# A transformer block with 4-bit FFN weights: attention ordered by rising row blocks over all heads, QKV by chunks of rows, twelve row blocks projected inside the attention loop

## The chip, the core and the metric

The kernel runs on one core of a Trainium2 chip. The metric is the device time of one execution in microseconds; lower is better. The core's engines, each with its own instruction stream that it works through in order, are TensorE (PE in the profile; its weight loads stand apart as PEld), VectorE (DVE), ScalarE (ACT) and GpSimd (POOL). SyncE (SP) issues all DMAs of this kernel, in one order; 16 DMA engines carry them out.

## The reference

One transformer block in fp32 on x of 2048 rows by 1024 columns: causal attention with 16 heads of 64, rotary positions, then a gated FFN (inner width 2752) whose weights are 4-bit codes with a table of 16 values and a scale for each 64 of them.

```python
q, k, v = (layernorm(x) @ W).reshape(2048, 16, 64)   # for each of Wq, Wk, Wv
q, k = rotary(q), rotary(k)
attn = softmax(where(causal, q @ k.T, -1e9) / 8)
x = x + layernorm((attn @ v) @ Wo)
Wg, Wu, Wd = (NF4[codes] * scales)                    # 64 values share a scale
x = x + layernorm((silu(layernorm(x) @ Wg.T) * (layernorm(x) @ Wu.T)) @ Wd.T)
```

## The kernel before

**Products of three.** An fp32 operand is split into a high part in TensorE's rounded fp32 type (ACT copies it) and a low part (DVE or POOL subtracts). `split` (L130) does both. A product is three matmuls: high by high, high by low, low by high. The 128x512 matmul is the unit of everything.

**Buffers.** SBUF is cut into tagged slots (L71): `hd`, `w`, `xc`, `pa` of 8 KB per partition, `pb`, `f4`, `pw` of 4 KB, `t2` and `ol` of 2 KB, so many of each; a tile waits until a slot of its tag is free. The eight PSUM banks have tags too (L72): one `F` for QKV and projection, three `S` for scores, two `T` for maxima, row sums and transposes, one `O` and one `L` for the attention output and its low-part sum. A planning pass puts each engine's instructions in order by priority and readiness; the function `chain` (L333) fixes the order of TensorE's matmuls by hand through the whole attention loop.

**Start, 0 to about 190 us.** `make_x` (L197) normalises and transposes the four chunks of 512 rows of x into resident tiles and stores them to DRAM (`xd`). `prep_qkv` (L217) loads and splits the weight columns of a pair of heads `m`; pairs 0 and 1 are computed here for all four chunks. `qkv(m, c)` (L222) is a group: for each of q, k, v 24 matmuls into `F`, a copy, then rotary for q and k (DVE shuffle L251, multiply L252, POOL L253 and L254) or four transposes for v, the split, and a store to DRAM.

**The attention loop, about 190 to 1630 us.** It has 640 steps. A step is one unit `(h, J, kb)`: head `h`, query block `J` of 512 rows, key block `kb` of 128. Order (L286): head by head, `J` rising inside a head; only for the last pair of heads is `J` outside. In each step, in this order: `probabilities` (L373; two score matmuls into `S`, on the diagonal a mask matmul, exp on ACT, the split into `pw`, POOL's addition into `acc`), one `maxima` chunk (L341; a score matmul into `T`, DVE's maximum) for a block some 16 steps ahead, a share of filling matmuls, and `weighted` (L401; matmuls into `O` and `L`) for the unit two steps before. At a block's end the two banks are added (L415, L416) and stored to `at`, and the row sums follow by two matmuls. K and V of a head lie in two sets of tiles; `load_block` (L305) adds only the new 512 rows for each `J`.

The filling (`rest`, L490) is a generator: the groups of pairs 2 to 7, each reading its x chunk again from `xd` (`load_x`, L210), with the next pair's weights split along the way; then the output projection of the first four row blocks (`project`, L450: load `at`, multiply by the reciprocal sums, split, 48 matmuls, and `residual`, L475: layernorm, sum with x, layernorm, stores `x1d` and `yd`). A `GAP` ends a step's share. At most 6 matmuls a step are taken, 3.35 on average.

**Between loop and FFN, about 1630 to 1866 us.** `project_now` projects the other twelve row blocks; between them `fill_x2` loads finished blocks from `yd` and transposes them into the FFN's input tiles, and the first gate and up weight tile is decoded (`looked_up`, L574).

**FFN, from about 1866 us.** For each of 22 weight tiles 4 chunks of products, while DVE and ACT decode the next tile; then the down projection and the last residual.

Of the kernel before, what the change touches and what calls it, by code (L numbers as in the profile page):

```python
# [20 lines left out]
S = 2048  # L21
# [9 lines left out]
BESIDE = 4  # L31
NEWX = 7
EARLY = 1000
STEP = 4
PACE = 3.35
MOST = 6
LAG = 2
AHEAD = (16, 16, 18, 20)
LOADS = 4
# [19 lines left out]
def block_kernel(ctx, tc, x, wq, wk, wv, wo, gu_codes, gu_scales, d_codes, d_scales, cos_sin, out):  # L59
# [117 lines left out]
    def prep_w(w, m, scale, tag="w"):  # L177

        wf = slot("f4", [P, KE, P], F32, "wf")
        load(wf, w[:, m * P : (m + 1) * P].rearrange("(k p) n -> p k n", p=P))  # L180
        n = KE // 2 if tag == "pb" else KE
        parts = []
        for k0 in range(0, KE, n):
            t = slot(tag, [P, 2, n, P], FR, "w")
            for k in range(0, n, STEP):
                src, hi, lo = wf[:, k0 + k : k0 + k + STEP], t[:, 0, k : k + STEP], t[:, 1, k : k + STEP]
                A.activation(hi, src, AF.Copy, scale=scale)
                if m > 1:
                    V.scalar_tensor_tensor(lo, src, scale, f32(hi), ALU.mult, ALU.subtract)
                else:  # L190
                    if scale != 1.0:
                        G.tensor_scalar(src, src, scale, 0.0, ALU.mult, ALU.add)
                    G.tensor_tensor(lo, src, f32(hi), ALU.subtract)
            parts += [t[:, :, k, :] for k in range(n)]
        return parts

    def make_x(c):  # L197
        tiles = [slot(("pa", "xc", "hd", "xc")[c], [P, 2, 2, 512], FR, "xr") for _ in range(4)]
        for t in range(4):
            r = (4 * c + t) * P  # L200
            xt = slot("hd" if c == 0 or t == 3 else "pw", [P, E], F32, "xt")
            load(xt, x[r : r + P, :])
            mean, rs, _ = ln_stats(halves(xt))
            V.tensor_scalar(xt, xt, mean, rs, ALU.subtract, ALU.mult)
            transposed(xt, tiles, slice(t * P, (t + 1) * P))
        for kp in range(4):
            load(xd[c][:, kp], f32(tiles[kp]))
        return tiles
# [8 lines left out]
    def prep_qkv(m, tags=("w", "w", "w")):  # L217
        return [prep_w(w, m, sc, tag) for w, sc, tag in zip((wq, wk, wv), (0.125, 1.0, 1.0), tags)]
# [3 lines left out]
    def qkv(m, c, ws, xs, ramp=False, following=None):  # L222

        cs = slice(c * 512, (c + 1) * 512)
        tab = slot("f4", [P, 2, 512], F32, "tab")
        load(tab, cos_sin[:, :, cs])
        for n in range(3):
# [8 lines left out]
            A.copy(t1, o)  # L236
            if following:
                following[n] = prep_w((wq, wk, wv)[n], m + 1, (0.125, 1.0, 1.0)[n])
            if n == 2:
                yield GAP  # L240
                pv = bank("F", "pv").rearrange("p (t n) -> p t n", t=4)
# [23 lines left out]

    xs = [early(make_x, 0)]
    first = [early(prep_qkv, 0), prep_qkv(1, ("pa", "pa", "pb"))]

    def new_x(c):
        xs.append(early(make_x, c))  # L270

    def both(*steps):
        for m, c in steps:
            for _ in qkv(m, c, first[m], xs[c], ramp=True):
                pass

    new_x(1)
    both((0, 0), (1, 0))
    new_x(2)
    both((0, 1), (1, 1))  # L280
    new_x(3)
    both((0, 2), (0, 3), (1, 2), (1, 3))


    last = KE - 1
    order = [(h, J) for h in range(2 * last) for J in range(NC)]  # L286
    order += [(h, J) for J in range(NC) for h in (2 * last, 2 * last + 1)]
    units, chunks, begin = [], [], {}
    for h, J in order:
        begin[h, J] = len(units)  # L290
        units += [(h, J, kb) for kb in range(4 * J + 4)]
        chunks += [(h, J, j, i) for j in range(4) for i in range(J + 1)]

    kv_of, q_of, q_free, pw_of, of, done = {}, {}, [], [], {}, set()

    def head_room():

        ka, kb = slot("hd", [P, S], FR, "ka"), slot("hd", [P, S], FR, "kb")
        va, vb = slot("hd", [P, NT, P], FR, "va"), slot("pa", [P, NT, P], FR, "vb")
        G.memset(f32(kb[:D]), 0.0)  # L300
        G.memset(f32(kb[:1]), 1.0)
        G.memset(f32(vb[:, :, D:]), 1.0)
        return ka, kb, va, vb

    def load_block(h, J):  # L305
# [3 lines left out]
        if h < 2 and J == 0:  # L309
            kv_of[h] = head_room()  # L310
        ka, kb, va, vb = kv_of[h % 2]
        for a in range(2):
            load(f32(ka[a * D : (a + 1) * D, cs]), ks[m][r : r + D, a, cs])
        load(f32(kb[D:, cs]), ks[m][r : r + D, 0, cs])
        if len(q_free) < 4 and not any(free for _, free in q_free):
            two = slot("pa", [P, 2, 2, 512], FR, "q")
            G.memset(f32(two[:D, :, 1]), 0.0)
            for i in range(2):
                q_free.append([two[:, i], True])
        entry = next(e for e in q_free if e[1])  # L320
        entry[1] = False
        q_of[h, J] = entry
        q = entry[0]
# [3 lines left out]
        ts = slice(4 * J, 4 * J + 4)  # L327
# [45 lines left out]
    def probabilities(u, h, J, kb):  # L373
# [9 lines left out]
        if kb == 4 * J + 3:  # L383
            q_of[h, J][1] = True
# [443 lines left out]
```

## Time and profile before

| what | value |
|---|---|
| time, median of 3 runs | 3258.65 us (3253.39 to 9025.56) |
| the profiled execution's time | 3266.51 us |
| its span, first to last instruction | 3264.5 us |
| mean granted TensorE clock | 0.965 |
| instructions | 42321 |
| DMA traffic | 569.68 MB, mean 175 GB/s |

Busy time counts the union of an engine's instructions. The heaviest groups of the attention part:

| line, engine | what | times | mean ns |
|---|---|---|---|
| L399 POOL | acc, sum of the high probabilities | 576 | 1144 |
| L353 DVE | row maxima | 640 | 603 |
| L132 DVE | low part of the probabilities | 640 | 603 |
| L385 ACT | exp | 640 | 518 |
| L131 ACT | high part of the probabilities | 640 | 524 |
| L189 DVE | low part of a weight half tile | 36 | 903 |
| L193 POOL | the same for the first two pairs | 12 | 1352 |
| L187 ACT | high part of a weight half tile | 48 | 632 |

DMA issues that the change touches, as the profile lists them: x chunks from `xd` 96 of 1024 KB; rotary tables 32 of 512 KB; weights 24 of 512 KB; `ka` 128, `kb` 64 and `vb` 64 of 128 KB, `va` 64 of 256 KB; x stores 16 of 1024 KB.

How to read it: an engine's row gives its name, busy time, share of the span and number of instructions. A table by stage gives the same for a stretch of time. A wait names who waited, for whom, the sum, how often, and the longest.

### The profile page before, as it was taken

Reading aid. Unit: us, or ns where it says so; the run is one execution under the profiler, and the core shown is the slowest. Engines: PE = TensorE matmul, PEld = TensorE weight load, DVE = VectorE, ACT = ScalarE, POOL = GpSimd, SP = SyncE. Lnnn points to the kernel's source line nnn. Section 1 sums busy time; section 2 is a strip of 40 time slices with the busy share of each in tenths; the row PEclk is TensorE's granted clock in tenths of the full one; section 3 lists DMA queues with packets and bytes.
Section 4 is the critical chain, followed back from the end, with each engine's and each line's share of the span. In section 5 each row is a group of like instructions: output and inputs, shape, how many; then the busy total and the mean of one; then the engine's idle time right before and its main releaser. Section 6 shows DMA issues by size and latency. Waiting matters only on the chain.

```text
span 3264.5 us, 42321 instructions
## 1 busy us (share of the span) xinstructions
PE 3027.4 (93%) x13760; PEld 2460.7 (75%) x13760; DVE 2232.7 (68%) x4037; ACT 1867.0 (57%) x3366; POOL 1008.7 (31%) x899
## 2 busy tenths in 40 slices
PE   8979999999998989968867999999999999999998
PEld 6857777777777767746656788888888888888887
DVE  8457777777777777756646598666677767957422
ACT  3246666666666656665625587555566556747311
POOL 5346666565665656664612100000000000000000
PEclk9989999999999999978978999999999999999999
DMA  8766757566566566453166533222222224868785
GB/s 304 262 194 199 239 157 219 182 186 213 183 190 207 189 180 216 149 142 91 57 174 194 180 117 115 92 97 97 104 97 100 91 99 153 299 206 254 257 290 206
DMA packets 307549, 569.68 MB, mean 175 GB/s; under 512 B 60160, under 2 KB 166656, under 8 KB 281728
## 3 DMA queue, kind: packets, MB, share of 16 engines
q1 hardware_dynamic: 307328, 566.99, 54.6%
q8 instruction: 108, 1.77, 0.2%
q14 instruction: 113, 0.93, 0.1%
HBM read 420.74 MB, written 146.15 MB: 174 GB/s over the span
## 4 chain that ended last, share of the span: by engine, by line
PE 74%; DMA 9%; DVE 8%; issue 4%; ACT 3%; POOL 2%; SPq 1%; DVEq 0%; POOLq 0%; ACTq 0%
PE bk L125 14%; PE bk L126 14%; PE bk L127 14%; PE qkv L232 4%; PE qkv L233 4%; PE qkv L234 4%; PE l L408 3%; PE mx L347 3%; PE o L407 3%; PE s L379 3%; PE s L380 3%; DMA rt<-rc 2%; DVE mxs L353 1%; DVE st L137 1%; DVE pw L132 1%
## 5 line engine op out<-in xcount | busy, mean ns | idle before, releaser
L399 POOL TENSOR_TENSOR acc<-acc,pw 128x512 f32<-128x512 f32 (+3 forms) x576 | 658.8, 1144 | 430.4 <-ACT pw L131 411.5
L591 ACT ACTIVATE ln<-cs,bias 128x512 f32<-128x512 f32 x910 | 611.4, 718 | 135.3 <-DVE mp L597 46.4
L125 PE MATMUL bk<-x,wt 128*128 128x512 f32 x1376 | 535.6, 390 | 0.6 <-DVE x L132 0.5
L126 PE MATMUL bk<-x,wt 128*128 128x512 f32 x1376 | 535.9, 390 | 0.0
L127 PE MATMUL bk<-x,wt 128*128 128x512 f32 x1376 | 535.6, 389 | 0.0
L143 POOL TENSOR_TENSOR rs<-ve,nhalf 128x1 f32<-128x1 f32 x64 | 40.5, 637 | 1560.0 <-DVE ve L141 1559.9
L353 DVE TENSOR_REDUCE mxs<-mx 128x1 f32<-128x512 f32 (+3 forms) x640 | 380.8, 603 | 190.0 <-PE mx L347 109.7
L385 ACT ACTIVATE s<-s 128x512 f32<-128x512 f32 (+3 forms) x640 | 330.7, 518 | 298.7 <-PE s L380 168.8
L132 DVE TENSOR_TENSOR pw<-s,pw 128x512 fp32r<-128x512 f32 (+3 forms) x640 | 383.5, 603 | 133.6 <-ACT pw L131 129.0
L131 ACT CAST pw<-s 128x512 fp32r<-128x512 f32 (+3 forms) x640 | 332.5, 524 | 33.2 <-POOL acc L399 3.1
L125 PEld LDWEIGHTS bk<-x,wt 128*128 128x128 f32 x1376 | 258.6, 188 | 54.7 <-issue 0.8
L126 PEld LDWEIGHTS bk<-x,wt 128*128 128x128 f32 x1376 | 258.7, 188 | 53.7 <-DVE x L132 0.3
L127 PEld LDWEIGHTS bk<-x,wt 128*128 128x128 f32 x1376 | 258.8, 188 | 53.7
L232 PE MATMUL qkv<-xc,w 128*128 128x512 f32 x576 | 238.8, 415 | 60.2 <-issue 42.2
L408 PE MATMUL l<-pw,vb 128*128 128x512 f32 (+3 forms) x640 | 247.0, 386 | 26.2 <-DVE acc L416 19.6
L125 PE MATMUL bk<-wd,it 128*128 128x512 f32 x672 | 261.7, 389 | 0.6 <-DMA it<-ind 0.5
L126 PE MATMUL bk<-wd,it 128*128 128x512 f32 x672 | 261.4, 389 | 0.0
L127 PE MATMUL bk<-wd,it 128*128 128x512 f32 x672 | 261.3, 389 | 0.0
L407 PE MATMUL o<-pw,va 128*128 128x512 f32 (+3 forms) x640 | 243.1, 380 | 16.3 <-ACT pw L131 9.9
L347 PE MATMUL mx<-ka,q 128*128 128x512 f32 (+3 forms) x640 | 246.0, 396 | 9.2 <-DVE mxs L353 6.1
L379 PE MATMUL s<-q,ka 128*128 128x512 f32 (+3 forms) x640 | 243.7, 381 | 3.7 <-DVE pw L132 3.6
L380 PE MATMUL s<-q,kb 128*128 128x512 f32 (+3 forms) x640 | 239.0, 373 | 0.0
(140 smaller groups left out, 5774.6 us busy)
## 6 DMA issues: line engine op xcount, KB each, us to landing
xc<-xd SPq DMA_DIRECT2D x96, 1024.0 KB
it<-ind SPq DMA_DIRECT2D x84, 1024.0 KB
ind<-hl SPq DMA_DIRECT2D x84, 512.0 KB
q<-qs SPq DMA_DIRECT2D x192, 128.0 KB
cs<-in_gu_scales SPq DMA_DIRECT2D x172, 128.0 KB
cs<-in_gu_codes SPq DMA_DIRECT2D x86, 256.0 KB
tab<-in_cos_sin SPq DMA_DIRECT2D x32, 512.0 KB
xd<-xr SPq DMA_DIRECT2D x16, 1024.0 KB
```

Source lines behind the costliest of these rows:

```text
L125: r = T.matmul(o, lhsT=w[:, 0], rhs=xx[:, 0], start=first, stop=False)
L126: T.matmul(o, lhsT=w[:, 0], rhs=xx[:, 1], start=False, stop=False)
L127: T.matmul(o, lhsT=w[:, 1], rhs=xx[:, 0], start=False, stop=last)
L132: V.tensor_tensor(lo, src, f32(hi), ALU.subtract)
L232: yield T.matmul(o, lhsT=w[k][:, 0], rhs=xx[:, 0], start=k == 0, stop=False)
L347: chain(T.matmul(s, lhsT=q[:, 0, j * P : (j + 1) * P], rhs=ka[:, b:e], start=True, stop=not diag))
L353: V.tensor_reduce(mx[:, j, i : i + 1], s, AX.X, ALU.max, negate=True)
L379: chain(T.matmul(s[:, cs], lhsT=ka[:, ks_], rhs=q[:, 0, cs], start=True, stop=False))
L399: G.tensor_tensor(acc[:, cs], acc[:, cs], f32(pw[:, 0, cs]), ALU.add)
L407: chain(T.matmul(o[:, cs], lhsT=va[:, kb], rhs=pw[:, 0, cs], start=kb == 0, stop=end))
L408: chain(T.matmul(ls[:, cs], lhsT=vb[:, kb], rhs=pw[:, 1, cs], start=kb == 0, stop=end))
L591: A.activation(ln, c8, AF.Identity, bias=bias_of[ab], scale=ab[0])
```

## The change

1. **Order of the loop.** `J` is outside for all heads: block 0 of the 16 heads, then block 1, and so on. K and V no longer stay with a head: each block loads its whole past into rings of tiles (`room`), three for `ka`, two each for `kb`, `va`, `vb`; `ka` with q from `load_q`, then `load_k` 8 and `load_v` 5 steps ahead of the block.
2. **QKV.** Groups run chunk by chunk. x of the current chunk stays in the `xc` slots and its rotary table in a `pw` slot. Weights are loaded and split again for every group; low parts of q's weights are subtracted on DVE, those of k's and v's on POOL. The factor 1/8 moves from q's weights to the copy of q. The start makes only x's first chunk and four groups; the other three chunks are made between the loop's steps by a second generator, `other_x`, with its transposes in `chain`, and reach the loop through DRAM. The transposes of v go to bank `T`.
3. **Filling.** 28 groups and the projections of twelve row blocks, at the rate of the table `FILL` (step, matmuls by then), up to 16 in a step. A projection waits four gaps ahead of its matmuls, and its result `y` takes the slot of its input `af`.
4. **Units.** The split of the probabilities (`parts`) comes after the filling; `pw` has three places instead of four; the matmul into `L` goes ahead of that into `O`; 65 rows of `L` are copied by ACT and DVE adds from the copy.
5. **After the loop.** The last four row blocks are projected; the first two gate and up tiles run for chunks 0 and 1 ahead of chunks 2 and 3, whose x2 is filled in between.

```diff
-BESIDE = 4
+BESIDE = 12
-PACE = 3.35
-MOST = 6
+STARTUP = 4
+MOST = 16
+FILL = ((-12, 0), (14, 304), (130, 912), (290, 1520), (430, 2128), (440, 2128), (640, 2704))
...
+        for k in range(0, KE, STEP):
+            src, hi, lo = wf[:, k : k + STEP], t[:, 0, k : k + STEP], t[:, 1, k : k + STEP]
+            A.copy(hi, src)
+            (G if n else V).tensor_tensor(lo, src, f32(hi), ALU.subtract)
...
+    def x_rows(r, tag):
+        xt = slot(tag, [P, E], F32, "xt")
+        load(xt, x[r * P : (r + 1) * P, :])
+        mean, rs, _ = ln_stats(halves(xt))
+        V.tensor_scalar(xt, xt, mean, rs, ALU.subtract, ALU.mult)
+        return xt
...
+    def make_x(c, t):
+        xt = x_rows(4 * c + t, "f4")
+        for _ in range(3):
+            yield GAP
+        for g in range(0, KE, 4):
+            pt = bank("T", "pt").rearrange("p (k n) -> p k n", k=4)
+            for k in range(4):
+                yield T.transpose(pt[:, k], xt[:, (g + k) * P : (g + k + 1) * P], ident)
+            for k in range(0, 4, 2):
+                xs = slot("t2", [P, 2, 2, P], FR, "xs")
+                split(xs[:, 0], xs[:, 1], pt[:, k : k + 2])
+                load(xd[c][:, (g + k) // 2, :, :, t * P : (t + 1) * P], f32(xs))
+            yield GAP
...
-                pv = bank("F", "pv").rearrange("p (t n) -> p t n", t=4)
+                pv = bank("T", "pv").rearrange("p (t n) -> p t n", t=4)
...
-    order = [(h, J) for h in range(2 * last) for J in range(NC)]
-    order += [(h, J) for J in range(NC) for h in (2 * last, 2 * last + 1)]
+    order = [(h, J) for J in range(NC) for h in range(2 * KE)]
...
+    rings = {"ka": [3, 0, []], "kb": [2, 0, []], "va": [2, 0, []], "vb": [2, 0, []]}
...
+        ka = room("ka", h, J)
+        for a in range(2):
+            load(f32(ka[a * D : (a + 1) * D]), ks[m][r : r + D, a, : cs.stop])
...
+    def load_k(h, J):
+        m, r = h // 2, h % 2 * D
+        load(f32(room("kb", h, J)[D:]), ks[m][r : r + D, 0, : J * 512 + 512])
+
+    def load_v(h, J):
+        m, cs = h // 2, slice(0, J * 512 + 512)
+        load(f32(room("va", h, J)), vs[m][cs, h % 2, :].rearrange("(t p) n -> p t n", p=P))
+        load(f32(room("vb", h, J)[:, :, :D]), vs[m][cs, h % 2, :D].rearrange("(t p) n -> p t n", p=P))
...
+        if not pw_of:
+            two = slot("pa", [P, 2, 2, 512], FR, "pw")
+            pw_of.extend([two[:, 0], two[:, 1], slot("pb", [P, 2, 512], FR, "pw3")])
+        pw = pw_of[u % 3]
...
+        chain(T.matmul(ls[:, cs], lhsT=vb[:, kb], rhs=pw[:, 1, cs], start=kb == 0, stop=end))
         chain(T.matmul(o[:, cs], lhsT=va[:, kb], rhs=pw[:, 0, cs], start=kb == 0, stop=end))
-        chain(T.matmul(ls[:, cs], lhsT=vb[:, kb], rhs=pw[:, 1, cs], start=kb == 0, stop=end))
...
+        low = slot("ol", [D + 1, 512], F32, "low")
+        A.copy(low, ls[: D + 1, :])
         A.copy(y, o[D:, :])
-        low = slot("ol", [1, 512], F32, "low")
-        A.copy(low, ls[D : D + 1, :])
         V.tensor_tensor(y, o[:D, :], y, ALU.add)
-        V.tensor_tensor(y, ls[:D, :], y, ALU.add)
+        V.tensor_tensor(y, low[:D, :], y, ALU.add)
...
-        yield GAP
+        y = y if y is not None else af.rearrange("p k n -> p (k n)")
+        for _ in range(4):
+            yield GAP
...
+    groups = [(m, c) for c in range(NC) for m in range(KE)]
+
+    def other_x():
+        for c in range(1, NC):
+            while c > 1 and (0, c - 1) not in done:
+                yield GAP
+            for t in range(4):
+                yield from make_x(c, t)
+            done.add(("x", c))
...
+        for g in range(STARTUP, len(groups)):
+            m, c = groups[g]
+            if m == 0:
+                while ("x", c) not in done:
+                    yield GAP
+                xs_, tab_ = load_x(c), load_tab(c)
+                for _ in range(10):
+                    yield GAP
...
+    for n, (h, J) in enumerate(order):
+        b, nk = begin[h, J], 4 * J + 4
+        at_ = b - nk - 8
+        if n >= 4:
+            at_ = max(at_, begin[order[n - 4]] + 4 * order[n - 4][1] + 4)
+        put(at_, 0, load_q, n, h, J)
+        put(b - 8, 0, load_k, h, J)
+        put(b - 5, 0, load_v, h, J)
...
+        want = np.interp(step, *zip(*FILL))
...
+                if step < 20 or step % 3 == 0:
+                    while (mm := next(beside, GAP)) is not GAP:
+                        chain(mm)
...
+    for t in range(4):
+        fill_x2(t)
+        steps[t]()
+    for t in range(BESIDE, NT):
         project_now(t)
+        if t < BESIDE + 2:
+            fill_x2(2 * t - 2 * BESIDE + 4)
+            fill_x2(2 * t - 2 * BESIDE + 5)
...
+        if it < 2:
+            for c in range(2):
+                gate_up(*todo[it], c)
+        if it == 1:
+            new_x2(2, ["w"] * 3 + ["pa"])
+            new_x2(3, ["xc"] * 4)
+            for t in range(8, NT):
+                fill_x2(t)
+            for i in range(2):
+                for c in (2, 3):
+                    gate_up(*todo[i], c)
```

## The prediction

> **What bounds the kernel now.** I read the page's busy times first, then a table by stage, then TensorE's waits in each stage, then a few microseconds of the timeline for the price of one matmul.
>
> ```profile
> PE 3027.4 (93%) x13760; PEld 2460.7 (75%) x13760; DVE 2232.7 (68%) x4037; ACT 1867.0 (57%) x3366; POOL 1008.7 (31%) x899
> ```
>
> PE looks full, but its durations overlap, so this row can't say what is left. The stages do (columns: window, its length, busy us and instructions of PE, PEld, DVE, ACT, POOL, then granted clock, DMA share, GB/s):
>
> ```profile
> 0.00:190.00 190.00, 166.26 (x769) 135.47 (x769) 116.87 (x261) 57.35 (x135) 86.04 (x91) 0.98 0.82 275
> ...
> 300.00:1390.00 1090.00, 1008.86 (x4863) 811.46 (x4862) 819.59 (x1444) 716.31 (x1431) 672.41 (x587) 0.97 0.63 192
> 1390.00:1628.00 238.00, 187.40 (x774) 140.13 (x773) 145.78 (x262) 143.54 (x266) 133.28 (x114) 0.86 0.33 98
> 1628.00:1866.00 238.00, 182.49 (x794) 148.02 (x794) 134.03 (x272) 101.96 (x171) 47.46 (x40) 0.87 0.63 184
> 1866.00:3264.00 1398.00, 1389.05 (x6126) 1149.50 (x6124) 941.77 (x1667) 781.66 (x1236) 9.18 (x16) 1.00 0.46 157
> ```
>
> The reader is to see one full stage, the FFN from 1866 us at clock 1.00, and two poor ones before it at 0.86 and 0.87. The FFN has 6208 matmuls of 512 columns in 1398 us: 0.225 us each. The timeline prices narrow ones by the distance of starts:
>
> ```profile
> 708.08 0.28 PE L347 MATMUL mx<-ka,q 128*128 128x256 f32 x1
> 708.19 0.22 PE L349 MATMUL mx<-mask_q,ident_r 128*128 128x128 f32 x1
> 708.25 0.44 PE L234 MATMUL qkv<-xc,w 128*128 128x512 f32 x1
> ```
>
> 0.11 us for 256 columns, 0.06 for 128. So pure TensorE work is: a QKV group (72 matmuls, 4 transposes) 16.4 us. An attention block has five matmuls for each unit; its four diagonal units are 512 to 128 columns wide (5 x 1280 / 512 x 0.225 = 2.81), with 8 masks, 4 row transposes (12 x 0.058 = 0.70) and 2 sums (0.45): 3.96; each J adds four full units, 4.51. All 64 blocks take 686 us, 1.07 for each unit. A projected row block (48) is 10.8, the FFN 1399. All 32 groups, 64 blocks and 16 projections with 256 transposes make 1400, yet the FFN begins at 1866: **466 us idle, all before it**. By stage: to 190 us 8 groups and 128 transposes, 139 of work, 51 idle. 190 to 1390: 544 units and 24 groups, 978 of work, 222 idle. To 1628: 96 units and 4 projections, 146, 92 idle. To 1866: 12 projections and 128 transposes, 137, 101 idle. TensorE's waits name them; from 300 to 1390 us:
>
> ```profile
> PE qkv L232 <- issue: 40.7, 17, 4.6
> PE l L408 <- DVE acc L416: 16.8, 20, 2.0
> PE o L407 <- DVE acc L415: 5.7, 6, 1.8
> ```
>
> and from 1390 to 1866 us:
>
> ```profile
> PE pj L469 <- ACT a L131: 36.4, 4, 14.7
> PE pt L159 <- DMA y<-yd: 13.2, 6, 5.3
> PE pt L159 <- DVE mv L139: 13.1, 1, 13.1
> ```
>
> The first falls on a group's first matmul and has no engine as releaser. I take it for the x chunk, since SP's own queue shows the loads held until the group before has let go:
>
> ```profile
> SPq L214 <- PE qkv L234: 67.9, 40, 8.1
> ```
>
> **What the Trainium skill says.** "Perfetto Trace Analysis", Identifying the Most-Contended Engine: matmul busy share is no measure of what is left. Agreed: 93% busy, 466 us idle. "TensorE: Matmul & The Clock Gate", Part 1: an idle window of about 3.4 us halves the clock. The trace agrees in direction: 0.86 where waits reach 14.7 us, 1.00 in the FFN. "SBUF — State Buffer", Who interferes with whom: a DVE operation with two SBUF inputs contends with GpSimd's reads. Agreed: L252 takes 1055 ns beside a busy POOL, DVE's like operations in the FFN 685. The change gives POOL more, so I keep the loop's long durations.
>
> **The change, part by part.** TensorE's work stays 2.8 ms; what can move is the 466.
>
> *Start.* Four groups and 32 transposes instead of eight and 128: 68 us of work. The first-data waits stay; of 51 idle I keep 37. Loop from about 105 us (bounds 90, 130).
>
> *The loop's work.* 686 + 28 x 16.4 + 12 x 10.8 + 96 transposes (6) = 1283 us on PE.
>
> *Waits removed.* x is resident and loaded three times more: 43 us (row L232 in that window) go. The sum's bank is left by one copy instead of two DVE adds, and its matmul goes ahead of the other: 22 us go. So 157 of 222 stay, 16% of the work; on 1283 that is 205. Loop 1488.
>
> *DMA.* x loads fall from 96 of 1 MB to 12, tables from 32 of 0.5 MB to 4, x stores from 16 to 12 MB (in 48 pieces). Weights rise from 24 of 0.5 MB to 96, K and V from 64 x 0.77 to 160 x 0.77 MB, as a block now loads its whole past. -84 -14 -4 +36 +74 = +8 MB of 567. SP issues change by -84 -28 +72 +32 = -8. I cost it at nothing: it hides behind the loop's free third of DMA, and kb is asked for 8 steps (some 17 us) ahead, where the longest landing on the chain of waits was 13.1 us. Lose that cover and each late block costs some 4 us, up to 100.
>
> *POOL and ACT.* Weights are split for every group. Low halves of K and V move to POOL: 28 x 4 x 1.352 = 151 us. POOL in the loop: 703 (acc) + 160 (rotary) + 151 + 63 (wo, residual) = 1077. ACT: exp 331, cast 333, block ends 187, groups 28 x 7.6 (three copies of 0.59, two casts of 0.62 and two of 0.38, six weight casts of 0.63), projections 56, x and wo 26: 1145. Both under PE; queueing is their only price.
>
> *DVE.* pw 384, maxima 382, block ends 155, groups 28 x 8.0 = 224 (two each of shuffle 0.74, L252 1.06, low part 0.90, v's low 0.41 and a weight's low 0.90), twelve x blocks at 4.6 (two statistics of 0.68, normalising 1.17, four lows of 0.41, small ones 0.4), twelve projections at 6.4 (1.39, 1.22, four statistics, small ones 1.1): 1277 us, as much as PE. Before it had 820 of 1090 us, 75%.
>
> *Waits added.* PE's order is fixed, so whatever is placed early stops all behind it, attention's s, o and l too, and with them ACT and DVE. (a) The next projection: y now sits in af's slot, so the four f4 slots hold y and x1 until the residual is done. Before, the last y copy (1498.8 us) to the second normalise's end (1512.5) took 14; plus the low split, 16 us. Six steps (one for the copy, one for the residual, four gaps) at 1.6 us cover 10: 6 us x 11 hand-overs = 66. Bounds 0 and 176 (cover gone). (b) x transposes between steps, the second user of bank T, one pb slot, one acc slot fewer: 0 to 60, I take 20. Loop 1574.
>
> *Tail.* Work: 4 projections and 128 transposes, 50 us. Idle: the last sums to the first projection took about 27 us before; then DVE must make two weight tiles (28 each, from L586 to L604 and the split), 16 x2 fills (26) and four projections (26), of which 95 us come before the second tile is there, against PE's 69 to that point: 27; the second half of x2, 11. Together 115 us (85 to 150).
>
> Sum: 105 + 1574 + 115 + 1399 = 3193, against the profiled span of 3264.5 (2 us less than that execution's time, 3266.5): -71 us. The median of the runs is 3258.65, so **3187 us**.
>
> **Rivals.**
>
> *DVE is the bound (slower).* DVE and PE now ask for equal time, and in-order queues with three s banks gave DVE no more than 75% before. At 75.2%, 1277 us take 1698; 105 + 1698 + 115 = 1918 against 1866: +52, 3311 us, and more where x blocks and POOL's larger share stretch it. It decides from a loop of 1646 us, DVE below 77.6%. For it: DVE's maxima and pw rows lie on every unit's path. Against: DVE's pw and maxima rows waited 231 us in that window, nearly all for ACT and PE, so it wasn't the limit.
>
> *Almost all overlaps (much faster).* If the remaining 16% halves, for x's stalls also cost clock (0.97), and the hand-overs are covered, the loop is 1283 x 1.08 + 30 = 1416: -229, about 3030; at two thirds of that, 3100.
>
> *The gain is handed back.* The hand-over is wholly exposed: 1488 + 176 = 1664, total 1884: +18, 3277. Speaks for it: L469 waited 36.4 us in four visits. Against: there the loads came late through SP.
>
> *It doesn't do what it says.* If L232's wait was the single F bank and not x, 50 us stay: 3237.
>
> **How the numbers follow.** My forecast 0.40, its own range 3140 to 3235; much faster 0.20; handed back or not removed 0.13; DVE 0.27. About 2% (3193 and 3324) is what a measurement of this kernel tells from no change. Of my forecast 0.24 lies below 3193, with the 0.20: faster 0.44. The rest of it, the 0.13 and 0.05 of DVE's mild end: within 2% 0.34. Slower 0.22. The range of 3080 to 3320 cuts a tenth at each end and takes in the hand-over's bounds.
>
> **What would show it.** Loop from 90 to 130 us; L232's idle gone but for three chunk changes; L408 waiting for no DVE add; weights' low halves on POOL; waits on L469's successor of about 6 us, twelve times; DVE above 78% of the loop; FFN full from about 1795 instead of 1866. Wrong if DVE stays at 75% or less, if PE waits on K, V or weight DMAs, or if the clock of the loop falls below 0.97.

## The result, and the profile after

| kernel | time, us | ratio to before, 95% interval |
|---|---|---|
| before | 3258.33, median of 4 | |
| changed | 3461.07 (3448.96 to 3463.94), median of 4 | 1.062 [1.059, 1.066] |

The change makes the kernel 203 us slower; the forecast was 71 us faster. One execution of the kernel before, of 9025.56 us, is not counted in the ratio. The profiled execution's span is 3462.1 us, its mean TensorE clock 0.942. The page's busy row and the clock of 40 slices, then the table by stage (columns as before):

```profile
PE 3055.7 (88%) x13760; PEld 2480.3 (72%) x13760; DVE 2293.6 (66%) x4065; ACT 1937.7 (56%) x3510; POOL 1179.4 (34%) x1011
...
PEclk9899999999999998888788599999999999999999
```

```profile
0.00:105.00 105.00, 83.80 (x354) 68.76 (x355) 47.98 (x90) 34.42 (x71) 63.39 (x65) 0.97 0.74 203
105.00:300.00 195.00, 148.67 (x708) 120.83 (x708) 105.25 (x211) 87.16 (x191) 82.81 (x78) 0.85 0.69 201
300.00:1307.00 1007.00, 921.40 (x4432) 734.96 (x4431) 775.45 (x1346) 664.26 (x1349) 703.78 (x591) 0.98 0.77 195
1307.00:1898.00 591.00, 423.16 (x1756) 334.45 (x1756) 339.35 (x586) 305.50 (x545) 302.70 (x247) 0.83 0.52 130
1898.00:2068.00 170.00, 103.13 (x448) 84.50 (x448) 96.24 (x180) 75.47 (x122) 17.57 (x14) 0.78 0.40 122
2068.00:3462.00 1394.00, 1375.57 (x6066) 1136.83 (x6064) 929.31 (x1655) 770.88 (x1237) 9.17 (x16) 0.99 0.46 158
```

Three stages are too long: QKV with attention (to 1307 us), attention with the twelve projections (to 1898) and the tail (to 2068, from where the FFN runs almost without gaps; its first matmul starts at 2021). The clock is 0.83 and 0.78 in the latter two, and also 0.85 at the beginning of the first, from 105 to 300 us. For what follows, **idle** is counted by starts: the distance from one matmul's start to the next less its price at full clock (0.227 us for 512 columns, the median distance of starts in the FFN, and in proportion for fewer), put down to the later matmul's line. A low clock is therefore in it. The counts that the expectations quote differ from these by up to 5 us.

| stage | forecast | measured |
|---|---|---|
| to 105 us | 105 | 105 |
| idle, 105 to 1307 | 170 (16% of 937 of work, 20 for x) | 265 |
| idle, 1307 to 1898 | 122 (16% of 350, 66 for hand-overs) | 241 |
| tail, length | 115 | 170 |
| FFN, length | 1399 | 1394 |

The three excesses, about 95, 119 and 55 us, make up the 269 between the forecast span of 3193 and 3462. Of the 265 us some 80 lie before 300 us, 30 of them at L223, the x transposes. TensorE's waits name the last two at once, first from 1307 to 1898 us, then from 1898 to 2068:

```profile
PE pj L496 <- DVE a L131: 111.1, 11, 17.5
PE pj L494 <- ACT a L130: 13.7, 2, 10.4
```

```profile
PE pj L494 <- ACT a L130: 57.0, 2, 53.9
```

Eleven of the twelve projections keep TensorE waiting some 10 us for the low part of their own input, `a`, and one in the tail keeps it 53.9 us. From 105 to 1307 us no row is as large. The first is that of the x transposes, with one wait of 14.2 us; the others are in small pieces:

```profile
PE pt L223 <- DVE xt L192: 24.9, 4, 14.2
PE l L430 <- DVE pw L131: 22.3, 18, 3.3
PE mx L367 <- DVE mxs L373: 13.5, 14, 2.6
```

One hand-over on the timeline (start, length, engine, line, operation, in brackets the idle before it and its releaser):

```profile
1605.02 0.60 ACT L497 COPY af<-pj 128x512 f32<-128x512 f32 x1
...
1612.87 2.38 POOL L506 TENSOR_TENSOR x<-x,af 128x1024 f32<-128x1024 f32 x1 [1.67 <-PE mx L367]
...
1621.37 1.24 ACT L151 ACTIVATE af<-x,nb,rs 128x1024 f32<-128x1024 f32 x1 [3.70 <-DVE nb L144]
...
1621.47 0.51 SPq L507 DMA_DIRECT2D x1d<-x  x1
...
1627.20 1.22 DVE L131 TENSOR_TENSOR a<-af,a 128x1024 fp32r<-128x1024 f32 x1 [5.87 <-DMA x1d<-x]
1628.48 0.80 PE L496 MATMUL pj<-wo,a 128*128 128x512 f32 x1 [13.02 <-DVE a L131]
```

The next projection's low part needs the f4 slot of x1, which is held until x1's store has landed: 23.5 us from the last copy to the first matmul that needs that part, of which 13.0 are waited. The forecast had 16, and six steps to cover 10 of them. The cover is as forecast; the chain is longer. The second normalise (ACT's line), where the forecast's chain ended, ends 17.6 us after the copy instead of 14, and the store, which is issued 6.2 us behind POOL's sum, lands some 4.6 us later still.

### The profile page after: what moved, and what is told of

Its sections match the earlier page's. It is cut to its first block, busy times and chain, and to the rows that moved or that the text cites. A ratio compares the mean times of both kernels' runs of the same rounds, so it can differ in the third digit from the quotient of the medians.

```text
span 3462.1 us, 42790 instructions
## 1 busy us (share of the span) xinstructions
PE 3055.7 (88%) x13760; PEld 2480.3 (72%) x13760; DVE 2293.6 (66%) x4065; ACT 1937.7 (56%) x3510; POOL 1179.4 (34%) x1011
## 2 busy tenths in 40 slices
DMA packets 484066, 576.03 MB, mean 166 GB/s; under 512 B 109184, under 2 KB 363136, under 8 KB 467968
## 4 chain that ended last, share of the span: by engine, by line
PE 61%; DMA 14%; DVE 12%; ACT 5%; issue 4%; POOL 2%; SPq 2%; DVEq 0%; POOLq 0%; ACTq 0%
PE bk L125 11%; PE bk L126 11%; PE bk L124 11%; PE qkv L238 3%; PE qkv L240 3%; PE qkv L239 3%; PE mx L367 3%; PE l L430 2%; PE o L431 2%; PE s L401 2%; PE s L402 2%; DMA wf<-in_wv 2%; PE pj L496 2%; PE pj L494 2%; DVE mxs L373 2%
## 5 line engine op out<-in xcount | busy, mean ns | idle before, releaser
L422 POOL TENSOR_TENSOR acc<-acc,pw 128x512 f32<-128x512 f32 (+3 forms) x576 | 676.4, 1174 | 377.7 <-ACT pw L130 356.3
L238 PE MATMUL qkv<-xc,w 128*128 128x512 f32 x768 | 314.3, 410 | 2.5 <-ACT t L245 1.6
L239 PE MATMUL qkv<-xc,w 128*128 128x512 f32 x768 | 311.7, 406 | 0.0
L240 PE MATMUL qkv<-xc,w 128*128 128x512 f32 x768 | 310.3, 404 | 0.0
L367 PE MATMUL mx<-ka,q 128*128 128x512 f32 (+3 forms) x640 | 253.9, 398 | 37.6 <-DVE mxs L373 18.1
L430 PE MATMUL l<-pw,vb 128*128 128x512 f32 (+3 forms) x640 | 245.9, 384 | 44.8 <-DVE pw L131 33.9
```

The lines of the kernel that those rows point to most:

```text
L238: yield T.matmul(o, lhsT=w[k][:, 0], rhs=xx[:, 0], start=k == 0, stop=False)
L239: yield T.matmul(o, lhsT=w[k][:, 0], rhs=xx[:, 1], start=False, stop=False)
L240: yield T.matmul(o, lhsT=w[k][:, 1], rhs=xx[:, 0], start=False, stop=k == KE - 1)
L367: chain(T.matmul(s, lhsT=q[:, 0, j * P : (j + 1) * P], rhs=ka[:, b:e], start=True, stop=not diag))
L422: G.tensor_tensor(acc[:, cs], acc[:, cs], f32(pw[:, 0, cs]), ALU.add)
```

## The experiments

Times of the changed kernel's variants are medians of two runs unless said otherwise; an interval is about 0.5% of the time to each side, so differences under some 20 us are read from the traces, not from times.

### The hand-over and the tail

**e1_x1: x1 out of the f4 slots.** x1 goes as two halves into t2 slots, with its loads, addition, stores and normalising by halves.

```diff
...
-        residual(t, y, slot("f4" if beside else "pb", [P, E], F32, "x1"))
+        residual(t, y, [slot("t2", [P, 512], F32, "x1") for _ in range(2)] if beside else slot("pb", [P, E], F32, "x1"))
```

> Based on the changed kernel (3461 us). In the projections inside the loop the residual's tile x1 takes two t2 slots (2 KB each, idle by then) instead of an f4 slot; the sum with x, its store and the second normalise go by halves. Theory S (a slot: the next block's low part has to wait until x1 is stored and let go): TensorE's waits at the third matmul of a projection (L496's line, 124 us of idle between 1307 and 1898 us) fall to below 40 us, the clock of that stretch rises from 0.83 towards 0.93, and the time falls by 80 to 130 us, to about 3330 to 3380. Rival D (the distance: loads of the next block and its multiplication come too late whatever the slots): waits move to the first matmul of a projection (L494's line) and the time stays within 30 us of 3461.

Measured: 3377.8 us, ratio 1.038 [1.033, 1.044], 83 us less. The last unit ends at 1809 instead of 1894 us and the clock of its stage is 0.90 instead of 0.83. The waits of TensorE, then of DVE, from 1307 to 1810 us:

```profile
PE l L430 <- DVE pw L131: 61.3, 27, 7.6
PE pj L494 <- ACT a L130: 13.1, 2, 10.8
```

```profile
DVE af L486 <- DMA af<-at: 47.4, 7, 9.4
```

Of L496's row 1.1 us are left: a low part that no longer shares x1's slot doesn't wait for it. (The halves shorten the chain too; no run parts that from the slot.) A smaller wait takes its place: DVE works in order, stands at its product for the load of `af`, and the probabilities' low parts queue behind it.

**e3_gaps: ten gaps instead of four ahead of a projection's matmuls.**

```diff
-        for _ in range(4):
+        for _ in range(10):
```

> Based on the changed kernel (3461 us). Ten gaps instead of four ahead of a projection's matmuls, so that the hand-over has twelve steps instead of six. Theory S says that x1 is let go some 23 us after the last matmul: twelve steps of 1.6 to 2 us cover it, waits at the projections' third matmul fall from 124 us to below 40, and the time by 60 to 120 us; the burst of 16 matmuls in a step that follows may give some of it back. Rival D is also content with this one, but expects it to gain more than the x1 edit.

Measured: 3409.1 us, ratio 1.048 [1.042, 1.053]. L496's idle falls from 124 to 24 us, the last unit ends at 1839. Cover alone takes away most of this wait, without a slot; L430's idle rises to 68 us from 22, as in e1_x1 (72).

**e2_recip: the last reciprocals ahead of the lookups.** `reciprocals(3)` moves from the first projection behind the loop to just behind the loop's end.

> Based on the changed kernel (3461 us). After the loop the reciprocals of the last block's row sums are asked for ahead of the four table lookups of the first gate and up tile instead of behind them. Theory O (the two share the one ol slot, so the reciprocals stand behind four lookups): TensorE's longest wait after the loop (53.9 us at a projection's first matmul) falls to 10 to 20 us and the time by 30 to 45 us, to about 3415 to 3430. Rival: the FFN's first tile is the limit there (DVE's lookups), then the lookups end later by as much and the time stays within 10 us.

Measured: 3451.9 us, ratio 1.061 [1.056, 1.066]: no difference that the times can tell. The wait at L494 is still 46.2 us, so the reciprocals' place was not it.

**e7_tail: projections ahead of the lookups.**

```diff
     for t in range(4):
         fill_x2(t)
-        steps[t]()
     for t in range(BESIDE, NT):
         project_now(t)
+        steps[t - BESIDE]()
```

> Changed kernel, but behind the loop each of the last four projections is issued ahead of one lookup step of x2's second half, and the fills of x2 come first. Theory O2 (the first projection behind the loop waits 53.9 us because its loads and DVE work stand behind four lookup steps on shared slots and queues): the wait on row L494 behind the last unit falls below 20 us, FFN begins 35-50 us sooner, time 3410-3428. Rival (it waits for the last blocks' own results, reciprocals among them): the wait stays above 40 us, time within 10 us of 3461.

Measured: 3414.8 us, ratio 1.049 [1.044, 1.055], 46 us less. TensorE's wait in the tail is 13.5 us where it was 53.9:

```profile
PE pj L494 <- ACT a L130: 19.5, 2, 13.5
```

### The stage with QKV

**e5_xgap: six gaps ahead of the x transposes instead of three** (in `make_x`).

> Changed kernel (3461 us), but the transposes of an x block come six gaps after its normalising instead of three. Theory P (the transposes, placed early in TensorE's fixed order, stand before x rows are there: row L223 waits 34 us from 105 to 1307 us): that row falls below 10 us, the time to 3415-3440. Rival (the x rows are late because DVE is late, and the wait only moves to the group's first matmul L238): L238's idle grows by what L223 loses, time within 10 us of 3461.

Measured: 3441.7 us, ratio 1.058 [1.052, 1.063]. From 105 to 1307 us L223's idle falls from 35 to 12 us, L367's rises from 42 to 53, L238's from 17 to 27: nearly all of the 23 us moved on to other lines, as the rival has it. QKV's last matmul still comes at 1281 instead of 1293 us, and the first FFN matmul at 2003 instead of 2021. The gain in time, 19 us, is at the edge of what these runs can tell.

**e6_pvF: v's transposes back in bank F**, `pv = bank("F", "pv")`.

> Changed kernel, but the four transposes of a v tile go to bank F, which the QKV group itself uses, instead of bank T, which row maxima use at every step. Theory T (bank T's second user costs what stands at L367 and L252: 44 and 19 us of idle before them from 105 to 1307 us): the two fall by 30 us or more together, time 3420-3440. Rival (L367 waits for a maximum on DVE, not for the bank's other user; F must then be left before the next group's matmul): L367 stays above 35 us, time 3455-3480.

Measured: 3525.5 us, ratio 1.083 [1.078, 1.089], 64 us more. L367 falls from 42 to 33 and L252 from 20 to 10 us, so bank T's second user has its price; but L238, the next group's first matmul into the single bank F, rises from 17 to 97. The change was right to move them.

**e4_oswap: the matmul into O ahead of that into L again** (the two lines in `weighted` change places).

> Based on the changed kernel (3461 us). The matmul into O goes ahead of that into L again, the rest stays. Theory: with the split now behind the filling, the matmul into L stands first in line for DVE's low part, which is ready some 0.7 us after ACT's high part; turning them round gives back most of the 40 us idle before L (105 to 1307 us) and of the 22 us later: 20 to 50 us less. Rival: the idle time only moves from L to O, as the high part is late too: within 10 us of 3461.

Measured: 3465.8 us, ratio 1.065 [1.060, 1.070]. L430's idle falls from 40 to 25 us and L431's rises from 23 to 28; what is won there is lost elsewhere, and the time gains nothing.

**e9_parts: the probabilities split straight behind the exponentials.**

```diff
-        put(u, 5, parts, u, h, J, kb)
+        put(u, 5 if u >= 3 and units[u - 3][2] == 0 else 1, parts, u, h, J, kb)
```

> Changed kernel, but the split of a unit's probabilities is put ahead of the step's row maxima and of its QKV or projection copies, straight behind the exponentials, except where the tile of probabilities would still be read. Theory W (TensorE's waits at L430 and L431, 62 us from 105 to 1307 us, come because DVE makes the low part last in its step): the two fall below 30 us there, time 3410-3435. Rival (the step as a whole takes its time on DVE and ACT, what is put first delays the maxima and copies behind it): L367 and L238 rise by as much, time within 15 us of 3461.

Measured: 3445.7 us, ratio 1.059 [1.054, 1.064]. L430 and L431 together have 66 us of idle, 63 before the edit. The low part is not late for its place in the step.

**e13_most8: at most 8 filling matmuls a step from step 20 on.**

```diff
-                for _ in range(MOST):
+                for _ in range(MOST if step < 20 else 8):
```

> Changed kernel, but from step 20 on at most 8 matmuls of a QKV group or a projection stand between two attention steps instead of 16 (6 in the kernel before). Theory B (bursts of 16, 3.6 us of TensorE, leave ACT and DVE without attention work, and TensorE then waits for them at the maxima, the row sums and the probabilities): idle from 300 to 1307 us falls from 189 to about 140 us, time 3400-3425. Rival (the mean number in a step is what counts, 4 to 5, and bursts only follow gaps): idle stays above 175 us, time 3445-3470.

Measured: 3454.5 us, ratio 1.061 [1.056, 1.065]; idle from 300 to 1307 us is 187, no less than in the changed kernel (184). It isn't the bursts.

**e10_nocos: DVE's product with the cosine table left out** (line L261).

> Changed kernel without DVE's multiplication by the cosine table (L261): the rotary of q and k leaves that product out, 56 operations of 1.15 us in the loop, 64 us of DVE. Theory D (DVE, busy 73% from 105 to 1307 us, is as full as its in-order queue lets it be and sets that stage): the stage shortens by 60-85 us, time 3375-3405. Rival (DVE waits for row maxima and exponentials and has room; the stage is set by TensorE's order and the clock its waits cost): the stage shortens by 20 us at most, time 3440-3461.

Measured: 3443.1 us, ratio 1.059 [1.055, 1.062]. QKV's last matmul comes at 1278 instead of 1292 us: 64 us of DVE are worth 14. DVE is not the bound of this stage.

**e16_onew: no preparation of weights in the loop.**

```diff
-            following = [None] * 3
-            yield from qkv(m, c, w, xs_, tab_, following=(following, groups[g + 1][0]) if g + 1 < len(groups) else None)
+            yield from qkv(m, c, w, xs_, tab_)
             done.add((m, c))
-            w = following
```

> Changed kernel that leaves out the preparation of weights in the loop: all its QKV groups use the tiles of group 4, so 27 groups less of 1.5 MB loads, six ACT casts (0.63 us), four POOL and two DVE low halves (1.37 and 1.06 us): 102 us of ACT, 148 of POOL, 57 of DVE. Theory W2 (weights split anew for every group are the load that keeps the stage from 105 to 1307 us long): the stage shortens by 60 us or more, time below 3400. Rival (as with the cosine product, what the engines do beside attention is hidden, and the stage is set by TensorE's waits one by one): the stage shortens by 25 us at most, time 3435-3461.

Measured: 3377.0 us, ratio 1.037 [1.033, 1.040], 84 us less; QKV ends at 1214. This is the load. It leaves out all 81 weight tiles of the loop; the kernel before prepared 18 in its own, so what the change added costs somewhat less than 84 us. Tables over the same stretch, the kernel before first, then the changed one, then this one:

```profile
300.00:1214.00 914.00, 841.91 (x4035) 675.68 (x4034) 687.67 (x1207) 597.12 (x1193) 557.55 (x486) 0.97 0.64 196
```

```profile
300.00:1214.00 914.00, 833.44 (x4017) 665.21 (x4017) 703.37 (x1225) 601.88 (x1226) 634.32 (x535) 0.98 0.78 198
```

```profile
300.00:1214.00 914.00, 879.62 (x4316) 711.20 (x4315) 709.20 (x1266) 585.03 (x1180) 565.53 (x491) 0.99 0.67 170
```

Without the preparation TensorE starts some 300 more matmuls in the same time: idle is 114 us on 800 of work (14%), where the changed kernel has 174 on 740 (24%) and the kernel before had 165 on 749 (22%). No engine was full, and DVE's operations hardly lengthen beside POOL's larger share (row maxima 682 ns in the changed kernel and 683 in this one, the product with the cosine table 1182 and 1149). TensorE's wait for the low parts of the probabilities, 22.3 us from 105 to 1307 us in the changed kernel (shown above), shows the difference; from 105 to 1220 us in this one:

```profile
PE l L430 <- DVE pw L131: 4.6, 6, 1.6
```

DVE makes a low part from ACT's high part. ACT's waits from 300 to 1214 us were, first of the kernel before, then of the changed kernel:

```profile
ACT hl L131 <- POOL t L254: 12.0, 18, 1.6
```

```profile
ACT hl L130 <- POOL t L263: 35.8, 23, 3.6
...
ACT w L183 <- DMA wf<-in_wv: 22.3, 11, 4.4
...
ACT w L183 <- DMA wf<-in_wk: 7.9, 4, 3.1
```

ACT, in order, stands 66 us for weights' loads and for POOL's part of the rotary, against 12 before; exponentials and probabilities queue behind that. e16_onew still has 25.2 us for POOL and no row for weights: only some 10 of POOL's 36 us go with the preparation.

**e18_acthi: no low halves of weights in the loop.** `prep_w` skips the subtraction there and hands out the high half twice; loads and ACT's casts stay.

```diff
...
-            (G if n else V).tensor_tensor(lo, src, f32(hi), ALU.subtract)
+            if low:
+                (G if n else V).tensor_tensor(lo, src, f32(hi), ALU.subtract)
...
```

> Changed kernel in which the loop's groups use the high half of a weight in place of its low half, so that POOL and DVE make no low halves there (148 and 57 us), while the loads and ACT's casts (102 us) stay. Theory A (ACT's casts stand ahead of the exponentials and casts of the probabilities in its order, and they are the cost): QKV ends less than 25 us sooner than 1292 us, time above 3435. Rival P (POOL, which holds the sums of the probabilities, and DVE are the cost): QKV ends 50 us or more sooner, time below 3410.

Measured: 3405.4 us, ratio 1.046 [1.044, 1.048]; QKV ends at 1239, 53 us sooner. Of 78 us that e16_onew took from the stage, two thirds belong to the low halves, and most of those to POOL's 148 us, if DVE's 57 are worth here what e10_nocos's 64 were; the other 25 belong to ACT's casts with their loads, which no run parts. ACT's waits from 300 to 1214 us:

```profile
ACT hl L130 <- POOL t L264: 25.5, 20, 4.7
...
ACT w L183 <- DMA wf<-in_wk: 12.9, 6, 5.6
```

Loads and casts are those of the changed kernel, yet ACT waits 18.4 us for weights' loads here and 33.5 there (all three weights). By the code a load needs an f4 slot, and a weight holds one until its low halves are made; so part of POOL's price may come as late loads. How much takes which way isn't shown.

### Towards a version that wins

**e8_late:** e1_x1 with DVE's product and the split three gaps behind the loads' issue, and three gaps more before the matmuls.

> The kernel with x1 in two t2 slots (3378 us), and DVE's multiply and split of a projection three gaps after their loads are issued instead of at once, then three gaps more before the matmuls. Theory H (DVE, which works in order, stood 47 us at L486 for the loads of af and rt with the low parts of the probabilities queued behind it, which TensorE then waited for: 61 us on L430): DVE's wait for af falls below 15 us, L430's below 25 us in the stage of projections, time 3330-3350. Rival (the loads are held by slots, SP issues them later still, and the wait moves to the projection's first matmul): L494 waits 30 us or more, time 3365-3390.

Measured: 3371.1 us, ratio 1.036 [1.030, 1.041]: as e1_x1. DVE's wait for `af` is 53 us, no less than the 47 there, since the loads are issued later as well. That is the rival's time, though not its place: TensorE waits 50.1 us at L430 and not at a projection's first matmul.

**e11_pre:** e1_x1, e5_xgap and e7_tail together, and the next projection's `af` and `rt` loaded behind the split of the one before (`heads(t + 1)`), their product behind its first half. It also has six gaps ahead of a projection's split and three instead of four behind it.

> Changed kernel with x1 in two t2 slots, x transposes after six gaps, the last four projections ahead of the lookup steps, and the loads of the next projection's af and rt issued behind the split of the one before, their product behind its first half. Theory S (what is left of the projections' cost is the one chain of hand-over: sum of the single edits -84, -20, -46, and the DVE waits at L486 gone, -30 to -50): time 3260-3285. Rival (the attention steps between take the time anyway, so the stage of projections keeps its waits under other names, L430 first): time 3305-3330.

Measured: 3345.5 us, ratio 1.029 [1.025, 1.032]. The three single gains, 83, 20 and 46, come to 116 together with the early loads and the gaps. The time lies above both expected ranges; as the rival had it, waits remain under another name. One of them on the timeline:

```profile
1446.13 1.23 DVE L520 TENSOR_TENSOR af<-af,rt 128x1024 f32<-128x1024 f32 x1 [8.90 <-DMA af<-at]
...
1447.88 0.79 PE L368 MATMUL mx<-ka,q 128*128 128x512 f32 x1 [4.87 <-DVE mxs L374]
...
1448.47 0.63 PE L515 MATMUL pj<-wo,a 128*128 128x512 f32 x1
1448.90 0.63 PE L516 MATMUL pj<-wo,a 128*128 128x512 f32 x1
...
1451.70 0.58 ACT L406 ACTIVATE s<-s 128x512 f32<-128x512 f32 x1 [7.39 <-PE s L403]
```

DVE stands 8.9 us for one load, TensorE 4.9 us for DVE's maximum, ACT 7.4 us for TensorE's scores.

**e12_actq:** e11_pre with those loads issued from ACT's queue (`A.dma_start` in `heads`). **e14_headslate:** beyond that, asked for behind the first half, their product three gaps behind the residual. **e15_ypw:** e11_pre with `y` in a pw slot and `rt` in an f4 slot.

> The kernel of e11_pre (3345 us), but the loads of af and rt are issued from ACT's queue instead of SP's, where they stood behind K loads that waited 142 us for their ring. Theory Q (SP's order makes af late: DVE waits 62 us at its product, TensorE 61 us at L431): DVE's wait for af and rt falls below 25 us, the stage of projections shortens by 30-50 us, time 3295-3315. Rival (ACT now stands for the slot instead, with the exponentials behind it, or DVE waits for the store of y as before): time 3335-3360.

> The kernel of e12_actq, but the next projection's loads are asked for after the first half of the matmuls instead of behind the split, and their product comes three gaps after the residual, the split three gaps later. Theory Q2 (with the loads off SP, the store of y has landed by then and nothing in order waits for it): DVE's wait for af and rt below 10 us, time 10-25 us below e12_actq. Rival (the longer chain of the hand-over shows): TensorE waits at the projection's first matmul L514 inside the loop, time above e12_actq.

> The kernel of e11_pre (3345 us), but y has a pw slot of its own and rt an f4 slot, so that no f4 slot is held until a store has landed. Theory S2 (y in af's slot is the rest of the slot theory: af and rt are asked for late, DVE stands 62 us for them and TensorE behind DVE): DVE's wait for af and rt falls below 15 us, L431's idle from 60 to below 35 us, time 3290-3315. Rival (SP's queue stands for the K ring in any case, or acc now waits for y's pw slot): time 3335-3365.

Measured: 3361.2, 3351.0 and 3375.0 us (ratios 1.032 [1.029, 1.035], 1.029 [1.024, 1.034], 1.036 [1.031, 1.042]); none gains over e11_pre. In the first two DVE's wait for `af` and `rt` falls from 62 to 35 and 30 us, short of the 25 and 10 expected, and ACT stands for the store of `y` instead (37.5 and 30.2 us at the exponentials), which still holds the f4 slot of the next `af`. In the third DVE waits 40 us for `rt`, and SP stands 110.6 us in `af`'s issue for the previous projection's matmuls, which hold the slot now; its time lies above the rival's range too. What sets these last 150 us of idle in the stage stays open: three ways round the slot each gave a new holder.

**e17_stored:** e11_pre, but weights split in the loop are stored split and from then on loaded so.

```diff
...
+        if (m, n) in wd:
+            t = slot(tag, [P, 2, KE, P], FR, "w")
+            load(f32(t), wd[m, n])
+            return [t[:, :, k, :] for k in range(KE)]
...
```

> The kernel of e11_pre (3345 us), but weights split in the loop are stored split (24 tiles of 1 MB) and from there on loaded split: 19 of 27 preparations in the loop go from the engines, and DMA carries some 24 MB of stores and 30 MB of loads more. Theory E (the engines' work is the cost that onew removed): the stage from 105 to 1300 us shortens by 45-65 us, time 3280-3300. Rival M (it was the DMA traffic, share 0.77 in that stage): time 3345-3390, with TensorE waiting at L239 for weights.

Measured: 3310.6 us, median of four, ratio 1.016 [1.014, 1.018]. QKV ends at 1257 instead of e11_pre's 1288 us, although DMA carries 631 MB instead of 576 and its share from 300 to 1280 us rises from 0.76 to 0.87. The engines' work outweighs the traffic. The stage's gain of 31 us falls short of the 45 expected, and whether the larger loads and the stores took the rest isn't shown. This is the fastest variant of the changed kernel, still 1.6% above the kernel before.

## Why the prediction was wrong

**Right.** The start took 105 us. x's waits at a group's first matmul went: L238, the successor of L232, has 2.5 us of idle on the page where L232 had 60.2. The FFN took what was said, and DMA traffic grew by some 6 MB (8 forecast), though in 484,066 packets instead of 307,549. No load of K, V or weights stands among what TensorE itself waited for from 105 to 1898 us.

**"Both under PE; queueing is their only price", for POOL and ACT.** The step that failed first, at a cost of up to 84 us (e16_onew). The work was summed rightly per engine (POOL has 1089 us from 105 to 1898 us, 1077 were forecast) and compared with TensorE's; what it does to engines that work in order beside attention was set at nothing. So the waits that the change removed were replaced: from 300 to 1214 us idle is 24% of work against 22% before, and the forecast's 16% is reached only with the weights' preparation gone (14%). Loads of weights, set at nothing as well, have a part in it: ACT waits 33.5 us for them.

**"22 us go", for the L bank.** About 5 went. L430 and L431 wait 17.4 us for block ends from 105 to 1307 us, where L407 and L408 waited 22.5 from 300 to 1390: for ACT's copy (7.8) and DVE's addition from the other bank (9.6).

**"(a) The next projection", 66 us.** Mechanism right, size wrong. L496's idle is 124 us, because a hand-over took 23.5 us and not 16 while the cover was the 10 forecast: x1's store had to be issued behind others on SP and to land, and the forecast's sum ended with the normalise. That is 58 of the stage's 119 us of excess. L494, a projection's first matmul, for which the forecast had nothing, has 30 more; the other 31 are spread over attention's lines. Part of the idle is the slow clock, named as a sign (a loop below 0.97): matmuls that start no more than about twice their price apart lose some 50 us in this stage. e1_x1 (83 us) and e3_gaps (52) show the hand-over by two ways.

**The tail, 115 us.** It took 170. The forecast had 27 us from the last sums to the first projection; it took 64 (1895 to 1959 us). In the code four lookup steps stand ahead of that projection, which waited 53.9 us for its input. Reordering returns 46 (e7_tail).

**"(b) x transposes between steps", 20 us for all of it.** Those at L223 alone left 35 us idle, nearly all of it before 300 us; e5_xgap returned 19, at the edge of noise.

These four single edits return 84, 83, 46 and some 20 us, 233 of 269; e16_onew takes out more than the change added, and the others overlap when combined (e11_pre), so this is no exact split. A small error of reading: 0.225 us for a matmul is 1% too low, since the FFN's first matmuls start at 1832 us and some 80 of the 6208 lie ahead of 1866.

**The rivals.** "DVE is the bound" names 3311 us, nearest of all and still 150 us off; that is luck. DVE is busy 77% from 300 to 1307 us, but over the whole loop, 105 to 1898 us, 1220 of 1793, or 68%: less than the 75.2% it rested on. The loop is longer than its mark of 1646 us, but idle time of any cause can make it so. e10_nocos refutes the mechanism: 64 us less of DVE shorten the stage by 14. "The gain is handed back" had the right place and an exposed hand-over, bounded at 176 us (124 measured), but lacked the other three costs. No rival held an engine's side work to be what delays attention. Of the signs of being wrong two came true: DVE at 68%, and a clock of 0.85 and 0.83 in parts of the loop.

## What to carry to other kernels

Where engines work in order beside a chain of short dependent steps, price side work by what it delays and not by whether its engine has room: here 205 us of low halves on POOL and DVE, both under 80% busy, cost the stage 53 us. When a tile is moved into a shared slot, follow its release to the last reader, the store's landing included, and price each stall on TensorE twice: its length, and the slow clock behind it (some 2 us in the stop shown below). A removed wait is a gain only if the next latest input is early; look that one up first.

## What was not expected of the hardware

After the 4.87 us stop in e11_pre, starts of 512-column matmuls stood 0.43 us apart (1448.47, 1448.90) instead of 0.23, and 4.6 us after work resumed 0.23 again. The Trainium skill, "TensorE: Matmul & The Clock Gate", Part 1, has 426.7 ns for a cold array and about 3.4 us of busy time before it is warm: the trace agrees on the spacing, and its 4.6 us are somewhat more than 3.4. The changed kernel's stage from 1307 to 1898 us has 19 stops of over 3 us, and its granted clock is 0.83.

The change lets DVE add the L part from a copy in SBUF (L439) and no longer from its bank. The whole page's groups, of the kernel before, then of the changed one:

```profile
L416 DVE TENSOR_TENSOR acc<-l,acc 64x512 f32<-64x512 f32 x64 | 43.0, 672 | 3.9 <-ACT low L414 3.5
```

```profile
L439 DVE TENSOR_TENSOR acc<-low,acc 64x512 f32<-64x512 f32 x64 | 61.8, 966 | 2.3 <-ACT low L436 2.0
```

The same addition takes 966 ns instead of 672, where its neighbour L438, which still reads a bank, stays at 674: both of L439's inputs now lie in SBUF, beside a busy POOL. "SBUF — State Buffer", Who interferes with whom, states that such operations contend with GpSimd's reads, and the longer time agrees; the prediction named it for others and not for this one, which the change itself makes.
